# Transposes of the routing's and the self-attention's input, moved from the three PSUM banks of the products to the two banks of the probabilities' transposes

## The chip, the cores and the metric

The kernel runs on one core of one Trainium2 chip. The metric is the device time of one launch in microseconds; lower is better. Before the change it is 809.06 us, the median of three runs (808.92, 809.06 and 810.75).

## The reference

One layer of a network works on x of 64 sequences × 32 tokens × 256 features and adds three terms to it in turn. The normalisation `_layernorm` has no scale and no bias. All is in 32-bit floats.

```python
x = x + _L0_xattn_ref(_layernorm(x), ctx_512, ...)   # 16 heads of 64, 257 context rows of 128 per sequence
x = x + _L0_attn_ref(_layernorm(x), ...)             # 4 heads of 64 over the 32 tokens, half of a head rotated
x = x + _L0_ffn_ref(_layernorm(x), ...)              # 8 experts, the best 2 for each token

# in _L0_xattn_ref
scores = jnp.einsum('bhnd,bhmd->bhnm', qh, kh) * scale
attn = jax.nn.softmax(scores, axis=-1)
out = jnp.einsum('bhnm,bhmd->bhnd', attn, vh)
# in _L0_ffn_ref
scores_BSN = jnp.einsum('bsd,nd->bsn', x, Wr) + br
_, idx_BSK = jax.lax.top_k(scores_BSN + biases_N[None, None, :], K)
h_NM2H = jnp.einsum('md,ndh->nmh', x_MD, Wl1) + bl1[:, None, :]
y_NMD = jnp.einsum('nmh,nhd->nmd', jax.nn.silu(a_NMH) * b_NMH, Wl2) + bl2[:, None, :]
```

## The kernel before

The 2048 tokens are 16 tiles t of 128 tokens, four sequences b in each. A loop over the 64 pairs (t, b), called **rounds** here, does the cross-attention: round (t, b) transposes the probabilities of its own sequence (`probs_transposed`, tile `tp`, twice: j = 0 and j = 1), computes the scores of the next round's sequence (`cross_probs`, tile `s`, four times), and multiplies the transposed probabilities with the context (`cross_mix`, tile `pa`).

The rest of the work is cut into pieces by generators, and at six places of each round the table `steps` says which generator gives its next piece:

- **ahead** is `cross_queries`, for the queries of two later tiles: `pqh` (one product tile a piece, which ScalarE scales and copies to `qh`) and `of_heads` (a pair of product tiles `pq`, the first copied by VectorE in L277, the second by ScalarE in L275).
- **near** is `rest` of the tile before, **far** `rest` of the tile before that. `rest` runs the output of the cross-attention (`pov`, `po`), the normalisation, the self-attention (`trs`, `pqkv`, `trqk`, `pss`, `pot`, `apo`), another normalisation, and the routing (`trr`, `pr`, `pk`).

Both transposes that the change is about lie in the third round of a tile (b = 2). TensorE's order there, for an even t and an odd t, is

```
even t: tp(j=0)  pqh  s s  trr  tp(j=1)  s  pqh      s  trs  pr  pa  pq pq
odd  t: tp(j=0)  pqh  s s  trr  tp(j=1)  s  pq pq    s  trs  pr  pa  pq pq
```

`trr` is the transpose of the routing's input `xr` of tile t - 2, `trs` that of the self-attention's input `xn` of tile t - 1. In the first rounds (t = 1) there is no `trr` and no `pr` yet, and in the last two tiles there is no ahead.

The order of TensorE's and SyncE's instructions is the order in which the code issues them. The order on ScalarE, VectorE and GpSimd is chosen by a planner when the kernel is built, from its own estimate of times.

The eight PSUM banks are three groups, by the tag of a tile: `s` has three banks (the scores; L308), `t` two (`tp`, L330, and a product of the experts, L648), and `a` three, which `bank` (L168) gives out: all other products and transposes. A tile holds its bank until the copy or the arithmetic that reads it has ended. Within a tag a new tile takes the bank that came free first by the planner's estimate, so its first instruction on TensorE waits for whoever reads the tile that had this bank before. `transposed` (L187 to L192) takes a bank of `a`, transposes n blocks of 128 columns with the identity, and has ScalarE copy the result to SBUF (`xaT` for `trs`, `xrT` for `trr`). TensorE works through its instructions strictly in order: whatever waits there holds all that is behind it.

After the 64 rounds come the blocks of the experts: 6 early ones, which are interleaved with the last tiles' `rest`, and 28 late ones.

Of the kernel before, what the change touches and what calls it, by code (L numbers as in the profile page):

```python
# [9 lines left out]
FP = mybir.dt.float32  # L10
# [40 lines left out]
def block_kernel(  # L51
# [132 lines left out]
        nc.vector.tensor_scalar(xn, xs[t], mv[:, 0:1], rstd, ALU.subtract, ALU.mult)  # L184
        return xn

    def transposed(dst, src, n, name):  # L187

        pt = bank([n, P], f"tr{name}")
        for k in range(n):  # L190
            nc.tensor.transpose(pt[:, k, :], src[:, k * P : (k + 1) * P], ident)
        nc.scalar.copy(dst, pt)  # L192
# [188 lines left out]

    def self_attention(t, xn):
        xaT = wk.tile([P, 2, P], FP, tag="xaT", name=f"xaT{t}")
        transposed(xaT, xn, 2, f"s{t}")
        yield
        qkv = wk.tile([P, 3 * D], FP, tag="qkv", name=f"qkv{t}")
        for lo, hi in ((0, 512), (512, 768)):
            pq = bank([hi - lo], f"pqkv{t}_{lo}")
            for k in range(2):
                nc.tensor.matmul(  # L390
                    pq, xaT[:, k, :], awqkv_sb[:, k, lo:hi], start=(k == 0), stop=(k == 1)
                )
            nc.vector.tensor_tensor(qkv[:, lo:hi], pq, abqkv_bc[:, lo:hi], ALU.add)
        yield

        heads = qkv[:, : 2 * D].rearrange("p (h d) -> p h d", d=HD)
        x1, x2 = heads[:, :, 32:48], heads[:, :, 48:64]
        cb, sb = cos.to_broadcast([P, 2 * AH, 16]), sin.to_broadcast([P, 2 * AH, 16])
        x1s = wk.tile([P, 2 * AH, 16], FP, tag="x1s", name=f"x1s{t}")
        x2s = wk.tile([P, 2 * AH, 16], FP, tag="x2s", name=f"x2s{t}")  # L400
        tc.keep_in_program_order(nc.vector.tensor_tensor(x1s, x1, sb, ALU.mult))
        nc.vector.tensor_tensor(x2s, x2, sb, ALU.mult)
        nc.vector.tensor_tensor(x1, x1, cb, ALU.mult)
        nc.vector.tensor_tensor(x2, x2, cb, ALU.mult)
        nc.vector.tensor_tensor(x1, x1, x2s, ALU.subtract)
        nc.vector.tensor_tensor(x2, x2, x1s, ALU.add)
        yield
        qkT = wk.tile([P, 4, P], FP, tag="qkT", name=f"qkT{t}")
        transposed(qkT, qkv, 4, f"qk{t}")
        yield  # L410


        sc = wk.tile([P, 2, 2, SEQ], FP, tag="sc", name=f"sc{t}")
        mx = sm.tile([P, 2, 2, 1], FP, tag="amx", name=f"amx{t}")
        for par in range(2):
            pss = bank([2, SEQ], f"pss{t}_{par}")
            r = par * HD
            for hh in range(2):
                for b in range(4):
                    nc.tensor.matmul(  # L420
                        pss[b * SEQ : (b + 1) * SEQ, hh, :],
                        qkT[r : r + HD, hh, b * SEQ : (b + 1) * SEQ],
                        qkT[r : r + HD, 2 + hh, b * SEQ : (b + 1) * SEQ],
                        start=True,
                        stop=True,
                    )
            nc.vector.tensor_reduce(mx[:, par, :, :], pss, AX.X, ALU.max)
            nc.vector.tensor_tensor(
                sc[:, par, :, :],
                pss,  # L430
                mx[:, par, :, :].to_broadcast([P, 2, SEQ]),
                ALU.subtract,
            )
        scf = sc.rearrange("p a h s -> p (a h) s")
        pr = wk.tile([P, AH, SEQ], FP, tag="apr", name=f"apr{t}")
        nc.scalar.activation(pr, scf, AF.Exp, bias=zero, scale=QK_SCALE)
        sums = sm.tile([P, AH, 1], FP, tag="asums", name=f"asums{t}")
        nc.vector.tensor_reduce(sums, pr, AX.X, ALU.add)
        inv = sm.tile([P, AH, 1], FP, tag="ainv", name=f"ainv{t}")
        nc.vector.reciprocal(inv, sums)  # L440
        nc.vector.tensor_tensor(pr, pr, inv.to_broadcast([P, AH, SEQ]), ALU.mult)
        dg = diag[t % 2]
        for b in range(4):
            r = slice(b * SEQ, (b + 1) * SEQ)
            nc.vector.transpose(dg[r, :, r], pr[r, :, :])
        yield
        pot = bank([2, P], f"pot{t}")
        for h in range(AH):
            par, hh = h % 2, h // 2
            nc.tensor.matmul(  # L450
                pot[par * HD : (par + 1) * HD, hh, :],
                qkv[:, 2 * D + h * HD : 2 * D + (h + 1) * HD],
                dg[:, par * 2 + hh, :],
                start=True,
                stop=True,
            )
        oT = wk.tile([P, 2, P], FP, tag="oT", name=f"oT{t}")
        nc.scalar.copy(oT, pot)
        yield
        xb = wk.tile([P, D], FP, tag="xb", name=f"axb{t}")  # L460
        nc.gpsimd.tensor_tensor(xb, xs[t], abo_bc, ALU.add)
        po = bank([D], f"apo{t}")
        for k in range(2):
            nc.tensor.matmul(po, oT[:, k, :], awo_sb[:, k, :], start=(k == 0), stop=(k == 1))
        nc.vector.tensor_tensor(xs[t], po, xb, ALU.add)

        queue = nc.sync if t < NT - 2 else nc.gpsimd
        queue.dma_start(out=out[t * P : (t + 1) * P, :], in_=xs[t])

    def route(t, xr):  # L470

        nc.gpsimd.tensor_copy(xr[:, RW - 1 : RW], token[:, t : t + 1])
        xT = wk.tile([P, 2, P], FP, tag="xrT", name=f"xrT{t}")
        transposed(xT, xr, 2, f"r{t}")
        yield
        pr = bank([NE], f"pr{t}")
        for k in range(2):
            nc.tensor.matmul(pr, xT[:, k, :], wr_sb[:, k, :], start=(k == 0), stop=(k == 1))
        sc = sm.tile([P, NE], FP, tag="rsc", name=f"rsc{t}")
        nc.vector.tensor_tensor(sc, pr, br_bc, ALU.add)  # L480
        sel = sm.tile([P, NE], FP, tag="rsel", name=f"rsel{t}")
        nc.vector.tensor_tensor(sel, sc, bn_bc, ALU.add)
        top = sm.tile([P, 8], FP, tag="rtop", name=f"rtop{t}")
        nc.vector.max(top, sel)
        idx = sm.tile([P, 8], U32, tag="ridx", name=f"ridx{t}")
        nc.vector.max_index(idx, top, sel)
        idf = sm.tile([P, 2, 1], FP, tag="ridf", name=f"ridf{t}")
        nc.vector.tensor_copy(idf[:, :, 0], idx[:, 0:2])

        two = sm.tile([P, 2, NE], FP, tag="rtwo", name=f"rtwo{t}")  # L490
        nc.vector.tensor_tensor(
            two, expert_id2, idf.to_broadcast([P, 2, NE]), ALU.is_equal
        )
        both = sm.tile([P, NE], FP, tag="rboth", name=f"rboth{t}")
        nc.vector.tensor_tensor(both, two[:, 0, :], two[:, 1, :], ALU.add)
        nmx = sm.tile([P, 1], FP, tag="rnmx", name=f"rnmx{t}")
        nc.vector.tensor_reduce(nmx, sc, AX.X, ALU.max, negate=True)
        ex = sm.tile([P, NE], FP, tag="rex", name=f"rex{t}")
        nc.scalar.activation(ex, sc, AF.Exp, bias=nmx)
        nc.vector.tensor_tensor(ex, ex, both, ALU.mult)  # L500
        tot = sm.tile([P, 1], FP, tag="rtot", name=f"rtot{t}")
        nc.vector.tensor_reduce(tot, ex, AX.X, ALU.add)
        inv = sm.tile([P, 1], FP, tag="rinv", name=f"rinv{t}")
        nc.vector.reciprocal(inv, tot)
        ew = xr[:, D : D + NE]
        nc.vector.tensor_scalar(ew, ex, inv, None, ALU.mult)
        yield

        pk = bank([NE], f"pk{t}")
        nc.tensor.matmul(pk, before, both, start=True, stop=False)  # L510
        nc.tensor.matmul(pk, ones, seen, start=False, stop=True)
        at = sm.tile([P, 1, NE], FP, tag="rat", name=f"rat{t}")
        nc.vector.tensor_tensor(at[:, 0, :], pk, region[:, 0, :], ALU.add)
        nc.vector.tensor_tensor(seen, seen, both, ALU.add)
        nc.vector.tensor_tensor(two, two, at.to_broadcast([P, 2, NE]), ALU.mult)
        slot = sm.tile([P, 2], FP, tag="rslot", name=f"rslot{t}")
        nc.vector.tensor_reduce(slot, two, AX.X, ALU.add)
        slots = sm.tile([P, 2], U32, tag="rslots", name=f"rslots{t}")
        nc.vector.tensor_copy(slots, slot)
        for k in range(2):  # L520
            nc.gpsimd.indirect_dma_start(  # L521
                out=routed[:, :],
                out_offset=bass.IndirectOffsetOnAxis(ap=slots[:, k : k + 1], axis=0),
                in_=xr,
                in_offset=None,
            )
# [648 lines left out]
```

## Time and profile before

| what | before |
|---|---|
| median of the runs | 809.06 us |
| time of the profiled execution | 811.05 us |
| its span, first to last instruction | 809.3 us |
| mean granted TensorE clock | 0.994 |
| ScalarE copies `xaT` (from `trs`), `xrT` (from `trr`) | 16 each, median 372 and 368 ns |
| ScalarE copies `pt` (from `tp`) | 128, median 587 ns |
| VectorE and ScalarE copies `q` (from `pq`) | 32 each, median 684 and 586 ns |
| first and last `trs` matmul | 78.6 and 599.7 us |
| first and last `trr` matmul | 110.0 and 623.8 us |
| first and last `tp` matmul | 22.4 and 582.3 us |

How it is read: the span is the time between the first and the last instruction on the core; the run's time has a little more around it. An engine's busy time is the sum of its instructions. A matmul is shown from its start to the end of its result, and the next one starts before that end, so on TensorE the distance between two starts tells more than a duration. "PE" is the matmuls, "PEld" the loads of their stationary operand. A row of the waits says which instruction sat idle, and whose end released it.

### The profile page before, as it was taken

To read this page: it belongs to the slowest core of one execution; us is meant where nothing else is said; L and a number is where in the kernel's file an instruction comes from. 1 tells how busy PE (TensorE), PEld (TensorE's weight loads), DVE (VectorE), ACT (ScalarE), POOL (GpSimd) and SP (SyncE) were. 2 spreads that over 40 slices of the span, in tenths; PEclk is the share of its full clock that TensorE was granted. 3 is DMA by queue.
4 is the path that set the end of the run, shared out by engine and by line. 5 is a ranking of instruction groups with operands and counts; after the bars stand their busy time and mean duration, and the time that the engine had idled before them with its cause. 6 is when DMAs were issued, how large, how long until landed. Compare 5 with 4: busy or idle time off the path is not lost. (4 is left out here: it accounts for less than half of the span.)

```text
span 809.3 us, 15134 instructions
## 1 busy us (share of the span) xinstructions
PE 778.6 (96%) x5212; PEld 612.5 (76%) x5212; DVE 496.9 (61%) x2045; ACT 378.3 (47%) x1078; POOL 143.7 (18%) x195
## 2 busy tenths in 40 slices
PE   8899999999999999999999999999998999999994
PEld 7576777677767767777767777676677899999994
DVE  4657666766686677677677766768665734334332
ACT  3564555556465555556554555555435322222220
POOL 3001011120201011111101110121123313333332
PEclk9999999999999999999999999999999999999998
DMA  9440202021020202022020102020441495356321
GB/s 306 140 112 1 66 11 67 11 89 51 27 79 11 67 10 80 10 75 65 27 66 11 66 11 67 14 73 15 163 162 34 114 398 144 54 139 210 60 41 21
DMA packets 32735, 64.14 MB, mean 79 GB/s; under 512 B 5328, under 2 KB 23632, under 8 KB 31120
## 3 DMA queue, kind: packets, MB, share of 16 engines
q1 hardware_dynamic: 26128, 54.08, 19.8%
q0 software_dynamic: 6528, 9.06, 6.2%
q8 instruction: 43, 0.70, 0.4%
q14 instruction: 36, 0.29, 0.1%
HBM read 87.54 MB, written 13.16 MB: 124 GB/s over the span
## 5 line engine op out<-in xcount | busy, mean ns | idle before, releaser
L314 ACT ACTIVATE pr<-s,nmx 128x257 f32<-128x257 f32 x256 | 121.7, 479 | 110.1 <-DVE nmx L313 101.9
L313 DVE TENSOR_REDUCE nmx<-s 128x1 f32<-128x257 f32 x256 | 105.8, 421 | 70.3 <-PE s L309 69.7
L309 PE MATMUL s<-kv,q 128*128 128x257 f32 x512 | 142.8, 387 | 1.6 <-ACT pr L314 1.4
L342 PE MATMUL pa<-pt,kv 128*128 128x512 f32 x256 | 123.3, 604 | 5.3 <-ACT ov L366 5.3
L309 PEld LDWEIGHTS s<-kv,q 128*128 128x128 f32 x512 | 89.1, 192 | 16.1 <-ACT pt L336 3.0
L332 PEld LDWEIGHTS tp<-ident,pr 128*128 128x128 f32 x512 | 61.5, 144 | 30.4 <-issue 15.7
L321 DVE TENSOR_SCALAR pr<-pr,inv 128x256 f32<-128x256 f32 x256 | 82.3, 363 | 3.3
L521 POOL DMA_INDIRECT routed<-xr,rslots x32 | 32.9, 1027 | 283.6 <-DVE lastT L1006 215.9
L332 PE MATMUL tp<-ident,pr 128*128 128x128 f32 x512 | 80.2, 278 | 1.6 <-DVE pr L321 1.6
L345 ACT COPY cT<-pa 128x512 f32<-128x512 f32 x64 | 37.5, 585 | 89.3 <-PE pa L342 89.3
L336 ACT COPY pt<-tp 128x512 f32<-128x512 f32 x128 | 75.4, 590 | 6.3 <-PE tp L332 6.0
L342 PEld LDWEIGHTS pa<-pt,kv 128*128 128x128 f32 x256 | 46.1, 190 | 39.8 <-issue 28.3
L695 POOL DMA_INDIRECT out_x<-y_late,to_late x28 | 43.5, 1555 | 107.3 <-DMA out_x<-y_late,to_late 33.5
L285 PE MATMUL pqh<-xqT,xwq_sb 128*128 128x256 f32 x256 | 60.8, 381 | 0.8 <-ACT xqT L192 0.8
L375 PE MATMUL po<-xwo_sb,ov 128*128 128x256 f32 x256 | 60.3, 379 | 0.0
L375 PEld LDWEIGHTS po<-xwo_sb,ov 128*128 128x128 f32 x256 | 48.6, 190 | 6.6
L285 PEld LDWEIGHTS pqh<-xqT,xwq_sb 128*128 128x128 f32 x256 | 47.4, 190 | 7.9 <-ACT xqT L192 1.5
L314 ACT ACTIVATION_READ_ACCUMULATOR pr<-s,nmx 128x1 f32 x256 | 51.7, 202 | 0.0
L319 DVE RECIPROCAL inv<-sums 128x2 f32<-128x2 f32 x128 | 20.5, 160 | 44.3 <-ACT pr L314 44.0
L631 ACT COPY bxT_late<-pxT_late 128x256 f32<-128x256 f32 x28 | 10.4, 372 | 73.1 <-PE pxT_late L629 73.1
L390 PE MATMUL pqkv<-awqkv_sb,xaT 128*128 128x512 f32 (+1 forms) x128 | 43.9, 486 | 0.0
L350 POOL TENSOR_TENSOR xb<-x,xbo_bc 128x256 f32<-128x256 f32 x16 | 11.6, 726 | 165.8 <-issue 117.2
(259 smaller groups left out, 1284.0 us busy)
## 6 DMA issues: line engine op xcount, KB each, us to landing
lane<-in_wall SPq DMA_DIRECT2D x24, 1028.0 KB
lane<-in_wall SPq DMA_DIRECT2D x24, 640.0 KB
lane2a<-in_wall SPq DMA_DIRECT2D x10, 1028.0 KB
kv<-in_ctx_t SPq DMA_DIRECT2D x16, 514.0 KB
kv<-in_ctx_a SPq DMA_DIRECT2D x16, 512.0 KB
lane2b<-in_wall SPq DMA_DIRECT2D x10, 640.0 KB
xg_late<-routed SPq DMA_DIRECT2D x28, 132.5 KB
x<-in_x SPq DMA_DIRECT2D x16, 128.0 KB
```

The costliest lines, as they stand in the source:

```text
L285: nc.tensor.matmul(pq[:, mm, :], xwq_sb[:, k, m * P : (m + 1) * P], xqT[:, k, :], start=(k == 0), stop=(k == 1),)
L309: nc.tensor.matmul(s, qb[:, g * P : (g + 1) * P], kvT[:, b, :], start=True, stop=True)
L313: nc.vector.tensor_reduce(nmx, s, AX.X, ALU.max, negate=True)
L314: nc.scalar.activation(pr[:, g, :], s, AF.Exp, bias=nmx, accum_out=sums[:, g : g + 1])
L321: nc.vector.tensor_scalar(pr[:, i, :ML], pr[:, i, :ML], inv[:, i : i + 1], None, ALU.mult)
L332: nc.tensor.transpose(tp[:, g * P : (g + 1) * P], pr[:, g, j * P : (j + 1) * P], ident)
L336: nc.scalar.copy(pt, tp)
L342: nc.tensor.matmul(pa, kvA[:, b, j, :], pts[j], start=(j == 0), stop=(j == MC - 1))
L345: nc.scalar.copy(cT[:, :, b, :], pa.rearrange("p (h n) -> p h n", n=SEQ))
L375: nc.tensor.matmul(po, ov[:, m, :], xwo_sb[:, m, :], start=False, stop=(m == XH // 2 - 1))
L390: nc.tensor.matmul(pq, xaT[:, k, :], awqkv_sb[:, k, lo:hi], start=(k == 0), stop=(k == 1))
L695: nc.gpsimd.indirect_dma_start(out=out[:, :], out_offset=bass.IndirectOffsetOnAxis(ap=self.to[:, b : b + 1], axis=0), in_=y, in_offset=Non ...
```

## The change

`transposed` gets a flag `beside`. With it the tile is taken from the tag `t`, whose two banks so far served `tp` (and the experts' second product), and not from the three banks of `a`. The flag is set for `trs` and for `trr` where t < NT - 2, that is for the tiles 0 to 13; the two last tiles, and the transposes of the queries (`trq`) and of the rotated queries and keys (`trqk`), stay in `a`. The instructions themselves, their number and their order on TensorE stay as they are.

```diff
-    def transposed(dst, src, n, name):
-
-        pt = bank([n, P], f"tr{name}")
+    def transposed(dst, src, n, name, beside=False):
+
+
+        if beside:
+            pt = ps.tile([P, n, P], FP, tag="t", bufs=2, name=f"tr{name}")
+        else:
+            pt = bank([n, P], f"tr{name}")
         for k in range(n):
             nc.tensor.transpose(pt[:, k, :], src[:, k * P : (k + 1) * P], ident)
         nc.scalar.copy(dst, pt)
@@ self_attention
-        transposed(xaT, xn, 2, f"s{t}")
+        transposed(xaT, xn, 2, f"s{t}", t < NT - 2)
@@ route
-        transposed(xT, xr, 2, f"r{t}")
+        transposed(xT, xr, 2, f"r{t}", t < NT - 2)
```

## Prediction

> **What bounds the kernel.** I read the page's busy times first, then what TensorE waited for, then the order of time in the third round of three tiles. Columns of a wait: total us, times, longest.
>
> ```profile
> PE 778.6 (96%) x5212; PEld 612.5 (76%) x5212; DVE 496.9 (61%) x2045; ACT 378.3 (47%) x1078; POOL 143.7 (18%) x195
> ...
> PE pa L342 <- ACT ov L366: 5.3, 14, 0.4
> PE trr L191 <- DVE xr L184: 3.0, 3, 1.4
> ...
> PE pr L478 <- DVE q L277: 1.0, 5, 0.2
> ```
>
> TensorE is busy for 96% of the span and in every slice; the next engine has 61%. What shortens TensorE's own row of starts shortens the run, and little else does. Its named waits are few, and one of them concerns a bank that this change touches: `pr`, the routing's product, waits five times for VectorE's copy `q`, which it doesn't read. It can only wait for that copy because it gets the bank of the first `pq` of the same round. The row counts the matmul's idle time alone, so the size has to come from the starts.
>
> The third round of an odd tile (t = 3), start and duration in us, TensorE, then ScalarE, then VectorE:
>
> ```profile
> 147.58 0.38 PE L191 MATMUL trr<-ident,xr 128*128 128x128 f32 x2
> 147.80 0.60 PE L332 MATMUL tp<-ident,pr 128*128 128x128 f32 x4
> ...
> 150.36 0.38 PE L191 MATMUL trs<-ident,xns 128*128 128x128 f32 x2
> 150.94 0.61 PE L478 MATMUL pr<-wr_sb,xrT 128*128 128x8 f32 x4 [0.20 <-DVE q L277]
> 151.41 1.96 PE L342 MATMUL pa<-pt,kv 128*128 128x512 f32 x4
> ...
> 145.23 0.59 ACT L336 COPY pt<-tp 128x512 f32<-128x512 f32 x1
> ...
> 149.13 0.37 ACT L192 COPY xrT<-trr 128x256 f32<-128x256 f32 x1
> ...
> 150.32 0.61 ACT L275 COPY q<-pq 128x512 f32<-128x512 f32 x1
> ...
> 150.20 0.69 DVE L277 COPY q<-pq 128x512 f32<-128x512 f32 x1
> ```
>
> The same place in an even tile (t = 2), and in tile 14, where no queries are left to compute:
>
> ```profile
> 113.22 0.38 PE L191 MATMUL trs<-ident,xns 128*128 128x128 f32 x2
> 113.44 0.51 PE L478 MATMUL pr<-wr_sb,xrT 128*128 128x8 f32 x4
> 113.81 1.96 PE L342 MATMUL pa<-pt,kv 128*128 128x512 f32 x4
> ...
> 544.77 0.60 PE L332 MATMUL tp<-ident,pr 128*128 128x128 f32 x4
> ...
> 546.08 0.38 PE L191 MATMUL trs<-ident,xns 128*128 128x128 f32 x2
> ...
> 545.78 0.37 ACT L192 COPY xrT<-trr 128x256 f32<-128x256 f32 x1
> ```
>
> In the even tile `pr` starts 0.22 us after `trs` and `pa` 0.37 after that: 0.59 in all. In the odd tile it is 0.58 and 0.47, 1.05 in all. The copy of VectorE ends at 150.20 + 0.69 = 150.89, and `pr` starts at 150.94, 0.05 later: that is the wait, and the other 0.10 is that a `pr` which had to stop also finds its weights not loaded ahead. **The wait costs 0.46 us.** It comes back at the same distance, 72.7 us, in the tiles 3, 5, 7, 9 and 11 (the five times of the row).
>
> **The change, part by part.**
>
> *Nothing is added or taken away.* The same transposes, the same copies (368 and 372 ns) and the same order on TensorE. What changes is which tile waits for which.
>
> *Waits in `a` that go.* In the odd third round the tiles of `a` were `pqh`, `trr`, `pq`, `pq`, `trs`, `pr`, `pa`; now they are `pqh`, `pq`, `pq`, `pr`, `pa`. With three banks `pr` follows `pqh`, whose copy (L292) started at 146.91 and took 0.60: free for three microseconds. `pr` then starts 0.22 after `trs`, and `pa` wants to start at 150.36 + 0.59 = 150.95. It gets the bank of one of the two `pq`: VectorE's copy ends at 150.89, ScalarE's at 150.32 + 0.61 = 150.93. With the 0.05 from above that is 150.94 or 150.98. So the wait doesn't move to `pa`: 0.00 to 0.03 is left of it. Gain for one such tile 0.43 to 0.46; I take 0.45, the middle. Five times: 2.25 us.
>
> *Tile 13* has the same wait in a shorter form: `trs` at 513.69, `pr` at 514.00, `pa` at 514.46, 0.77 in all, so 0.18 over 0.59. VectorE's copy ends at 513.25 + 0.69 = 513.94, and `pa` would come at 514.28: 0.18 gained. *Tile 1* has no `pr`; there `pa` waits for VectorE's `q`: `trs` at 78.61, copy ending 78.18 + 0.69 = 78.87, `pa` at 78.92 in place of 78.61 + 0.22. Now `pa` gets the bank of `pqh`: 0.09 gained. In the even tiles there is no stall, and nothing to gain.
>
> *Waits in `t` that come.* The four tiles of a third round are now `tp`, `trr`, `tp`, `trs` in two banks, so the second `tp` waits for the copy `pt` of the first, and `trs` for the copy `xrT` of `trr`. Behind each of them on TensorE stands the whole rest of the round, so any lateness counts in full. For the second `tp`: the copy ends at 145.23 + 0.59 = 145.82, the transposes start at 147.80, so 1.98 us are in hand; in tile 2 the copy (from 107.62, 0.59) ends 1.98 before 110.19; in tile 14 (542.90 + 0.59 against 544.77) 1.28. Cost nothing; what hides it is the `pqh` and two `s` between. For `trs`: in tile 3 `xrT` ends at 149.50, 0.86 ahead of `trs`; in tile 2 at 111.17 + 0.37 = 111.54, 1.68 ahead. In tile 14 it ends at 545.78 + 0.37 = 546.15, and `trs` started at 546.08: with 0.05 for the signal it starts at 546.20, 0.12 late, the one place where a new wait shows. Cost 0.12. In tile 15 `trr` belongs to tile 13 and moves, `trs` to tile 14 and stays, so nothing there waits for `xrT` early. In the round after, `tp` takes the banks of the second `tp` and of `trs`, copied long before.
>
> *The planner's order.* The trace can't show how ScalarE and VectorE will be ordered afterwards. The nearest rows: `xrT` could slip behind the `pt` of the second `tp` and one exponential (0.60 + 0.50 + 0.23), about 1.3 us against 0.86 in hand, which would hold `trs` by 0.4 in six odd tiles, 2.6 us lost; or other small waits, such as the 14 of `pa` for `ov`, each 0.4, could get shorter or longer, which a gain of half of them (2.6) bounds on the other side. I take zero, since the copies in question stand in the order in which TensorE produces what they read and nothing they read comes later, and keep both ends for the range.
>
> **Sum:** 2.25 + 0.18 + 0.09 - 0.12 = 2.4 us off a span of 809.3, which gives 806.9. The profiled execution took 811.05 as a run, 2.0 over the median of the runs shown, with 1.75 of it outside the span; I take the difference and not the level from it: 809.06 - 2.4 = **806.7 us**. That is 0.30% off, exactly the 0.3% that a measurement of this kernel can about tell from no change, so this forecast is split evenly between "faster" and "same".
>
> A rule of the Trainium skill speaks against the change: the page "Perfetto Trace Analysis", section "Matmuls", wants independent groups to rotate through different PSUM banks, so that the copy of one overlaps the matmuls of the next. Putting four groups through two banks goes the other way for `t`; by that rule the time would rise, as the slower rival below has it. The 1.98 us in hand say that two banks suffice for this sequence, so I don't follow it.
>
> **Rivals.**
>
> *The gain is taken back within the round* (chance 0.15): the planner's bank for `pa` or the place of `xrT` on ScalarE makes TensorE wait as long as before. For it: the bank of `pa` comes free within 0.03 us of when it is wanted, and `xrT` has 0.86 in hand, under two exponentials. Against: all six odd tiles show the same distances. Time: 2.4 - 2.6, so 809.1 to 809.3.
>
> *The second `tp` waits for the first one's copy* (chance 0.12; the slower side). Place: the start of the second `tp` in the 14 third rounds from tile 2 to tile 15. It decides from the point where `pt` ends 1.98 us later than now (1.28 in the last two tiles). That takes a planner that puts `pt` behind `qh` and the first exponential: it would start where that ended, at 148.22 + 0.48 = 148.70, end at 149.29 and hold `tp` from 147.80 to 149.34, 1.5 us, 14 times 21 us: 806.7 + 21 = 828. Against it: in all rounds read, `pt` is the first thing that ScalarE does after the transposes it reads, with idle time behind it (1.09 before `qh`).
>
> *More goes than the one wait* (chance 0.09): the planner also shortens the waits for `ov`: 806.7 - 2.6 = 804.1 at most, half of that likely, 805.4.
>
> **Chances.** Forecast 0.64, between 806.2 and 807.3 (the bounds of `pa`'s wait, 0.03 times five, the 0.12, and a spread of the runs of some tenths). Faster by over 0.3%: half of it plus the rival with more, and a little for a base that lies low, 0.32 + 0.09 + 0.03 = 0.44. Slower: 0.12. Same: the rest, 0.44. The range from 805.3 to 809.4 holds the forecast, the case taken back, and half of the case with more, some 0.83.
>
> **What would show it.** Right: the row of `pr` waiting for VectorE's `q` is gone; in odd third rounds `pr` starts 0.22 after `trs` and `pa` 0.59 to 0.62; in tile 14 `trs` waits some 0.1 for ScalarE's `xrT`; the row of `pa` behind `ov` stays at 14 times 0.4. Wrong: a new row in which `tp` waits for ScalarE's `pt`, `trs` for `xrT` in more than one tile, or `pa` for `q`, or a busy TensorE whose late blocks start no earlier than before, relative to the same waits.

## The result and the profile after

The changed kernel takes 807.52 us, median of 11 runs, against 810.82 us for 11 runs of the kernel before. The ratio is **0.9971, 95% interval 0.9959 to 0.9984**: 0.29% faster, 2.4 us, where 2.4 us were forecast (806.7 us, from a base of 809.06). It is taken over the fast runs alone, and so leaves out one run of the kernel before, of 1110.98 us. The two medians lie 3.3 us apart, so the size of the gain is known to about 1 us.

The profiled execution has a span of 803.8 us, 5.5 less than before. That is more than the runs show, and the view of the time by stretches says why. A part lies at the start, which the change doesn't touch. Columns: stretch and its length, busy time (and instructions) of TensorE, weight loads, VectorE, ScalarE and GpSimd, TensorE's granted clock, share of the DMA engines, GB/s. First before, then after:

```profile
24.00:28.00 4.00, 3.65 (x12) 2.99 (x13) 1.60 (x6) 1.96 (x6) 0.00 (x0) 0.59 0.85 226
```

```profile
24.00:28.00 4.00, 4.00 (x29) 3.50 (x28) 3.05 (x11) 3.02 (x11) 0.00 (x0) 1.00 0.74 214
```

In the profile of before the clock was granted at 0.59 in these four microseconds, and 12 matmuls were done in place of 29. So the profiles are compared from a point behind it: from the first to the last `trs` matmul, before and after (median duration, then first and last start):

```profile
L191 PE MATMUL trs<-ident,xns x32: 272/273/273, 78.6 to 599.7; 128*128 128x128 f32 x32
```

```profile
L195 PE MATMUL trs<-ident,xns x32: 272/273/328, 75.9 to 594.2; 128*128 128x128 f32 x32
```

521.1 us before and 518.3 after: **2.8 us** less in this stretch. The other 2.7 of the 5.5 had been won before the first `trs`: 0.41 of 4 us make 1.6 of them, and where the rest arose isn't shown. Behind the last `trs` both executions take 209.6 us. (All lines of the code behind `transposed` are four higher in the changed kernel.)

The longest of TensorE's waits after:

```profile
PE pa L346 <- ACT ov L370: 5.2, 14, 0.4
```

The row of `pr` waiting for `q` is gone, and the one of `pa` is what it was. The rows left out differ from those of before by 0.2 us at most, and none is of `tp`, `trs` or `pa` waiting for a copy of the third round. The third round of tile 3 in order of time; TensorE, VectorE, then ScalarE:

```profile
144.93 0.60 PE L336 MATMUL tp<-ident,pr 128*128 128x128 f32 x4
...
147.50 0.38 PE L195 MATMUL trs<-ident,xns 128*128 128x128 f32 x2
147.72 0.51 PE L482 MATMUL pr<-wr_sb,xrT 128*128 128x8 f32 x4
148.09 1.12 PE L346 MATMUL pa<-pt,kv 128*128 128x512 f32 x2
...
147.34 0.68 DVE L281 COPY q<-pq 128x512 f32<-128x512 f32 x1
...
142.36 0.59 ACT L340 COPY pt<-tp 128x512 f32<-128x512 f32 x1
...
146.27 0.37 ACT L196 COPY xrT<-trr 128x256 f32<-128x256 f32 x1
...
147.46 0.61 ACT L279 COPY q<-pq 128x512 f32<-128x512 f32 x1
```

`pr` now starts 0.22 us behind `trs`, while VectorE's copy `q` still has 0.30 to go, and `pa` 0.37 behind that: 0.59, as in the even tiles. The order on ScalarE is the one of before, in the whole profile. `pt` ends 1.98 us ahead of the second `tp`, and `xrT` 0.86 ahead of `trs`, to the hundredth what was in hand before.

### The profile page after: what moved, and what is told of

Read it like the earlier page. It is cut to its first block, busy times and chain, and to the rows that moved or that the text cites. A ratio compares the mean times of both kernels' runs of the same rounds, so it can differ in the third digit from the quotient of the medians.

```text
span 803.8 us, 15150 instructions
## 1 busy us (share of the span) xinstructions
PE 774.1 (96%) x5212; PEld 609.9 (76%) x5212; DVE 495.8 (62%) x2045; ACT 377.9 (47%) x1078; POOL 143.6 (18%) x195
```

## The experiments

Four kernels move other tiles between the groups of banks, to see which move counts. Each gives one number from its profile, the stretch from the first to the last `trs`, and a ratio from its runs.

### Only `trs` moves, or only `trr`

```diff
 e1:  transposed(xaT, xn, 2, f"s{t}", t < NT - 2)      transposed(xT, xr, 2, f"r{t}")
 e2:  transposed(xaT, xn, 2, f"s{t}")                  transposed(xT, xr, 2, f"r{t}", t < NT - 2)
```

> Of the change only the self-attention's transpose (trs) moves to the two banks; the routing's (trr) stays in a. Measure: from the first to the last trs matmul, 521.1 us before and 518.3 us with the whole change. Theory (pr no longer takes the bank that VectorE's copy q frees): pr now follows trr in the banks of a, so the wait is gone as with the whole change: 518.2 us, ratio to before about 0.997, and no wait of pr for q in the five tiles. Rival (the gain is shared by the two transposes, because a is less crowded in general): about 519.7 us, ratio about 0.9985.

> Of the change only the routing's transpose (trr) moves; trs stays in a. Theory: the tiles of a in an odd third round are pqh, pq, pq, trs, pr, pa, so pr still follows the first pq in its bank and still waits for VectorE's q, five times: 521.1 us from the first to the last trs, ratio 1.000, although as many transposes moved as with trs alone. Rival (shared gain): about 519.7 us, ratio about 0.9985.

The lines of `trs`, with `trs` alone and then with `trr` alone:

```profile
L195 PE MATMUL trs<-ident,xns x32: 272/272/273, 76.8 to 595.0; 128*128 128x128 f32 x32
```

```profile
L195 PE MATMUL trs<-ident,xns x32: 272/273/273, 77.0 to 598.3; 128*128 128x128 f32 x32
```

`trs` alone: 518.2 us, ratio 0.9953 (0.9937 to 0.9969). `trr` alone: 521.3 us, ratio 1.0003 (0.999 to 1.0017). The same number of transposes moved in both, and one brings all and the other nothing, so the gain isn't a matter of how many tiles share `a`. (The ratio of `trs` alone lies a little below the 0.997 expected, which is just outside its interval; the stretch agrees. The last section shows that executions scatter by some 2 us ahead of it.) With `trr` alone the wait shows again, and a little longer. It isn't the wait that was expected: it ends with ScalarE's copy of the second `pq`, not with VectorE's of the first:

```profile
PE pr L482 <- ACT q L279: 1.5, 5, 0.3
...
148.74 0.38 PE L195 MATMUL trs<-ident,xns 128*128 128x128 f32 x2
149.43 0.58 PE L482 MATMUL pr<-wr_sb,xrT 128*128 128x8 f32 x4 [0.31 <-ACT q L279]
149.86 1.53 PE L346 MATMUL pa<-pt,kv 128*128 128x512 f32 x3
```

`pa` comes 1.12 us after `trs` here, against 1.05 before. That is 0.07 more, and over the six odd tiles 0.4 us are lost; 0.2 of it come back in tiles 14 and 15, which leaves the 0.2 us between 521.1 and 521.3.

### Neither moves, and `pr` does

```diff
-        pr = bank([NE], f"pr{t}")
+        if t < NT - 2:
+            pr = ps.tile([P, NE], FP, tag="t", bufs=2, name=f"pr{t}")
+        else:
+            pr = bank([NE], f"pr{t}")
```

(in the kernel before)

> Both transposes stay in a as before; the routing's product pr itself moves to the two banks (tiles 0 to 13). Theory: the bank of pr is all that counts, so the wait is gone without moving a transpose: 518.6 us from the first to the last trs (tile 1, which has no pr, keeps its 0.2), ratio about 0.997. Rival (it is the transposes that gain from their new banks): 521.1 us, ratio 1.000.

```profile
L191 PE MATMUL trs<-ident,xns x32: 272/273/273, 78.1 to 596.5; 128*128 128x128 f32 x32
```

518.4 us, ratio 0.996 (0.9945 to 0.9975). No transpose left its banks, and the gain is there. What the change does for the time is to keep `pr` off the banks of the two `pq`.

### The self-attention's scores too

The same reading names the next wait: `pa` of a tile's first round, 14 times behind ScalarE's `ov`, whose bank it gets. On top of the whole change:

```diff
-            pss = bank([2, SEQ], f"pss{t}_{par}")
+            if t < NT - 2:
+                pss = ps.tile([P, 2, SEQ], FP, tag="t", bufs=2, name=f"pss{t}_{par}")
+            else:
+                pss = bank([2, SEQ], f"pss{t}_{par}")
```

> The whole change, and the self-attention's scores (pss, two tiles in the first round of a tile) in the two banks too, for tiles 0 to 13. Theory (a wait on a bank is set by which tile held it before): pa of the first round then follows the queries' transposes and no longer the second pov, whose copy ov it waits for 14 times; that row goes, some 0.4 us each: 518.3 - 5.2 = 513.1 us from the first to the last trs, about 801.5 us as a run, ratio about 0.990. Rival (two banks are too few for four more tiles in that round: the tp of the next round waits for VectorE's work on pss): a row of tp waiting for VectorE, and 518 us or more.

That place, in the kernel before and then in this one, and the line of `trs` in this one:

```profile
94.55 0.38 PE L420 MATMUL pss<-qkT 64*32 64x32 f32 x32
95.30 1.99 PE L342 MATMUL pa<-pt,kv 128*128 128x512 f32 x4 [0.37 <-ACT ov L366]
```

```profile
91.67 0.38 PE L427 MATMUL pss<-qkT 64*32 64x32 f32 x32
91.98 1.98 PE L346 MATMUL pa<-pt,kv 128*128 128x512 f32 x4
...
L195 PE MATMUL trs<-ident,xns x32: 272/273/329, 75.9 to 588.3; 128*128 128x128 f32 x32
```

`pa` follows `pss` after 0.31 us and not after 0.75, the row of `ov` is gone, and no row of `tp` waiting for VectorE's work on `pss` has come. 512.4 us for the stretch, 800.83 us as a run, **ratio 0.9892 (0.9874 to 0.991)**: this kernel beats both. The row of the waits promised 0.37 a time, and `pa` comes 0.44 earlier; what the other 0.07 are isn't shown. 14 times 0.44 are 6.2 us, and 5.9 were gained: in the third round of tile 9 `pa` now starts 0.55 us behind `pr` (360.95 and 361.50) and not 0.36, with no row that says why.

### How far the new wait is from deciding

The slower rival was that the second `tp` would wait for the copy of the first. Three kernels let ScalarE make that copy several times over in the third rounds of tiles 2 to 15 (the same data again, so that the bank comes free later):

```diff
         nc.scalar.copy(pt, tp)
+        if j == 0 and b == 2 and t >= 2:
+            for _ in range(3):          # d1, after; 6 in d2 (after) and d3 (before)
+                nc.scalar.copy(pt, tp)
```

> The changed kernel, with ScalarE copying the first tp of each third round (tiles 2 to 15) three times more, so that its bank comes free later. A further copy takes 0.48 us behind another, 1.4 us in all, against the 1.98 us that lie between the copy and the second tp (1.34 in tiles 14 and 15). Theory (the new wait of the second tp is hidden by these 1.98 us): no wait in tiles 2 to 13, some 0.1 us each in the last two, so within 1 us of the changed kernel. Rival (the second tp already stands at the edge): 1.4 us in 14 rounds, some 20 us more.

> The same with six further copies; the last ones stand behind the scaling of qh and two exponentials. Theory: the bank comes free about 2.9 us after the second tp wants it, so tp waits in all 14 third rounds: some 40 us more than the changed kernel, about 845 us, and a row of tp waiting for ScalarE's pt. If the bank of tp did not matter: like the next run, the same copies in the kernel before.

> The kernel before with the same six further copies: the control. There the second tp has a bank of its own, so only the later copies of ScalarE count (xrT, and through it trs and pr, by 0.6 to 1 us a round): about 815 us, some 30 us less than the changed kernel with the same copies.

Three copies on the changed kernel: 812.99 us, ratio to before 1.0038 (1.0016 to 1.006). Six: 861.01 us, 1.0627 (1.0562 to 1.0692). Six on the kernel before: 826.5 us, 1.0213 (1.0166 to 1.026). The waits of `tp` for the further copies, with three and then with six:

```profile
PE tp L336 <- ACT pt L343: 3.7, 2, 1.9
```

```profile
PE tp L336 <- ACT pt L343: 31.5, 12, 2.6
...
PE tp L336 <- ACT xrT L196: 4.2, 2, 2.1
```

With three copies only two second `tp` wait, those of tiles 14 and 15. In tiles 2 to 13 none does, though in tile 3 the last copy ended 1.85 us later than the first (147.47 against 145.62) and 0.12 ahead of the second `tp`: what the forecast costed at nothing is hidden by the 1.98 us in hand, down to the last tenth. With six, all 14 wait, 31.5 + 4.2 = 35.7 us in all, **some 2.5 us a time**. (By the second row two of them end with the copy `xrT`, that is with the bank of `trr`.) In the control no `tp` waits for the copies.

The two runs differ by 861.0 - 826.5 = 34.5 us, where 30 had been expected, but this is a balance and not the price of the bank alone. The control has waits of its own, behind `pt`, `rsc`, `xrT` and `q`, 10.6 us more than the kernel before has in these rows. And with six copies on the changed kernel TensorE's clock was halved for 24 us between the first and the last `trs`, against 3.4 in the control. Half of that time is an estimate of what it cost at most, 12 and 1.7 us.

Both levels lie above what was expected, by 16 and 11.5 us. On the changed kernel the waits are less than the 40 us expected, and up to 12 us are the clock's; in the control its own waits are 10.6 us where 6 had been allowed. The rest of both stays open.

One expectation failed outright. With three copies the kernel was to be within 1 us of the changed one; by the two ratios to before, 1.0038 and 0.9971, it is some 5 us slower. Some 0.1 us of wait was foreseen in tiles 14 and 15, and it is 1.85 in each; a halved clock, in the last section, adds 2.8 in the profiled execution, the slowest of seven. A further copy also took 0.62 us and not 0.48. In tile 14 ScalarE did this:

```profile
540.18 0.59 ACT L340 COPY pt<-tp 128x512 f32<-128x512 f32 x1
540.80 0.59 ACT L343 COPY pt<-tp 128x512 f32<-128x512 f32 x1
542.10 0.48 ACT L318 ACTIVATE pr<-s,nmx 128x257 f32<-128x257 f32 x1 [0.71 <-DVE nmx L317]
...
542.56 0.58 ACT L343 COPY pt<-tp 128x512 f32<-128x512 f32 x1
...
543.49 0.59 ACT L343 COPY pt<-tp 128x512 f32<-128x512 f32 x1
```

The planner put only one further copy next to the first, and the other two behind an exponential each, of which the first waited for VectorE; `tp` started at 544.14, behind the last copy. The two tiles are those whose third round has no `pqh`; that this is the planner's reason isn't shown. That is the slower rival's mechanism as it was written down, a copy placed behind an exponential. It needs another planner's order than the change brought.

## Why the prediction was right

**The bound.** TensorE is busy for 96% of the span before and after, and what was taken out of its row of starts came out of the run, as far as the runs can tell: 2.8 us in the profile's stretch; 2.4 in the runs, whose interval, 1.3 to 3.3 us, holds it.

**The wait of `pr`, 0.43 to 0.46 a time, taken as 0.45.** It is the whole 0.46: `trs` to `pa` went from 1.05 to 0.59. What was left open was whether `pa` would catch what `pr` let go; in the round above VectorE's copy ends at 147.34 + 0.68 = 148.02 and `pa` starts at 148.09 without a wait. It was close, as forecast: ScalarE's `q` ends 0.02 ahead of `pa`. Five times, 2.3 us. The part of it put down to weights that aren't loaded ahead is borne out: in the even tile `pr`'s first load starts at 113.33, 0.11 us ahead of `pr`, and in the odd one at 150.94, together with `pr`. That the bank is the cause, and not the transposes' own place, is shown by the three kernels that moved one tile each.

**Tile 13, 0.18.** As worked out: `trs` to `pa` fell from 0.77 to 0.59. (So not all six odd tiles show the same distances, as the first rival's text has it; five do.)

**Tile 1, 0.09.** Undersized: the later matmuls of that `pa` moved another 0.10, so 0.18. It is the size of the 0.10 that the forecast had added for `pr` and left out here; that a late weight load is the reason here too isn't shown.

**Tile 14, a cost of 0.12.** The start of `trs` there, after:

```profile
539.52 0.60 PE L336 MATMUL tp<-ident,pr 128*128 128x128 f32 x4
...
540.89 0.44 PE L195 MATMUL trs<-ident,xns 128*128 128x128 f32 x2
541.17 0.51 PE L482 MATMUL pr<-wr_sb,xrT 128*128 128x8 f32 x4
```

From the second `tp` to `trs` 1.37 us, against 1.31 before, and to `pr` 1.65 against 1.52: 0.13 late at `pr`, for the copy `xrT` that ends at 540.84. It is the one place where a new wait shows, of the size forecast. With `trs` alone moved it isn't there (`trs` then follows a `tp` in its bank), but 0.1 us in 800 is nothing that runs can tell.

**The sum.** 2.3 + 0.18 + 0.18 - 0.1 = 2.6 of the 2.8 us in the stretch; about 0.2 more lies in the first round of tile 15 (`pss` and `pa`), and its cause stays open. The same 0.2 is gained there with `trr` alone, where `pr` still waits, so it isn't `pr`'s bank that brings it. That the runs give the forecast's 2.4 to the tenth is luck: their interval is 2 us wide, and the sum came out at 2.6 to 2.8.

**The rivals.** None came. The planner left ScalarE's order as it was, so neither the wait at `pa` nor the one at the second `tp` arose. The rule of the Trainium skill that spoke against the change ("Perfetto Trace Analysis", section "Matmuls": independent groups rotate through different PSUM banks) has a real price here, the 2.5 us that `tp` waits a time with six copies, but only from the point where the copy isn't done by the time the bank is wanted. With 1.98 us in hand two banks rotate as well as three in this kernel.

## What to carry to other kernels

When an engine waits for an instruction whose result it doesn't read, look for the buffer they share: the cure may be to move a third tile out of the rotation, and which one (here `trs`, and not `trr`) follows from writing the order of the tiles down and counting back by the number of buffers. The count names a candidate, not more: with `trr` alone it named the first `pq`, and the wait fell on the second. Before a tile goes to a smaller group of buffers, read how much time lies between the copy that frees the buffer and the instruction that wants it; where that is well over what the planner could shift, the smaller group cost nothing here.

## What the runs showed of the hardware

**TensorE's clock was halved near the start in some executions and not in others, for the same work.** Up to the first `trs` all nine profiled kernels do the same work. Five of them had a mean clock of 0.5 to 0.6 in the stretch from 24 to 28 us and reached the first `trs` at 78.1 to 79.6 us; the other four had not, and reached it at 75.9 to 77.0. The last big gap on TensorE ahead of it, 1.6 us of `tp` waiting for VectorE from 22 to 23 us on, is in all of them. That is about 2 us of scatter, as much as this change, and a reason to compare stretches behind it.

**Two short waits close together halved it in one tile and not in the next.** In the run with three copies, around the 0.92 us of `trr` and the 1.85 us of `tp` in tile 14:

```profile
540.00:544.00 4.00, 1.37 (x7) 0.71 (x6) 1.88 (x7) 3.26 (x10) 0.83 (x3) 0.91 0.07 19
544.00:546.00 2.00, 1.86 (x7) 1.67 (x8) 0.46 (x2) 0.95 (x3) 0.00 (x0) 0.50 0.00 0
546.00:550.00 4.00, 4.00 (x12) 2.68 (x11) 2.70 (x16) 1.70 (x6) 0.00 (x0) 0.50 0.00 0
```

TensorE was busy for 1.37 of four microseconds, and then ran at 0.50 for six. In tile 15 the same two waits come again, 0.91 and 1.85 us, the second up to 581.90, and the clock stays:

```profile
582.00:584.00 2.00, 2.00 (x15) 1.84 (x16) 1.08 (x3) 1.22 (x5) 0.00 (x0) 1.00 0.99 408
584.00:588.00 4.00, 4.00 (x16) 2.27 (x17) 2.59 (x18) 2.55 (x8) 0.00 (x0) 1.00 0.94 315
```

In tile 14, from this `tp` (544.14) to the next (550.77) it took 6.63 us, against 3.81 in the changed kernel (539.52 to 543.33): the clock cost 2.8 us on top of the 1.85 us wait. The Trainium skill's page "TensorE: Matmul & The Clock Gate", section "What's actually happening", has the clock halved after an idle window of some 3.4 us that runs freely and doesn't start with the kernel. This case agrees with such a window: in each of the nine traces the changes of the clock lie whole multiples of 3.413 us apart. It doesn't agree that the window has to be idle: no single gap here was longer than 1.85 us, and matmuls ran between the two. Where the waits fall among these steps fits the difference between the tiles. In tile 14 one step, 539.84 to 543.25, holds the first wait and half of the second, with TensorE busy for 1.53 of 3.41 us; in tile 15 they are spread over two steps, with 1.75 and 2.32. A threshold doesn't come out of it: with six copies, two steps with 1.36 and 1.40 us of work were followed by the full clock.
